# LSTM with a residual: 114 single-pass full-array matmuls on a tile of zeros, and element operations on that tile

## The chip, the core and the metric

The kernel runs on one core of a Trainium2 chip. The metric is the device time of one execution in microseconds (us). The core has five engines that run their own instruction streams and wait for each other by semaphores: PE (TensorE, matrix products into the PSUM memory), DVE (VectorE), ACT (ScalarE), POOL (GpSimd) and SP (which issues most DMA transfers here). PEld is PE's weight load, which can run beside its matmuls.

## The reference

An LSTM over T = 512 steps for a batch of 32, with 512 inputs and 512 hidden units; its output is added to its input. All data are float32.

```python
xW = jnp.einsum('ntd,dg->ntg', x, Wx) + b
def step(carry, xw_t):
    prev_h, prev_c = carry
    a = xw_t + prev_h @ Wh
    i = sigmoid(a[:, :Hd]); f = sigmoid(a[:, Hd:2*Hd]); o = sigmoid(a[:, 2*Hd:3*Hd])
    g = tanh(a[:, 3*Hd:])
    next_c = f * prev_c + i * g
    next_h = o * tanh(next_c)
    return (next_h, next_c), next_h
...
x = x + lstm(x, h0, Wx, Wh, b)
```

## The kernel before

The steps of the recurrence depend on each other, so the kernel is one loop over t = 0 to 511. The batch of 32 fills only 32 of the 128 columns of PE's array; four products, one for each quarter of the hidden units (j = 0 to 3), therefore run side by side, each in its own group of 32 columns, and write 32 of the 128 partitions of a PSUM bank of 512 float32 columns. Each such f32 product shows in the trace as two records of a matmul and two of a weight load.

In step t, `h_part(t)` (L201 to L212) adds h times Wh to the bank of that step: 4 slices of h times 4 quarters, 16 products of 512 columns. `cell(t)` (L214 on) then applies the gates: ACT reads the bank (L225 to L227) and computes tanh of c (L232), DVE forms c and h (L229, L230, L234) and transposes h (L236) into `ht`, one of two buffers, which the next step's `h_part` reads. POOL adds x to `ht` (L244) into `oc`, a tile with room for two steps; every second step SP stores it (L248). In the last eight steps DVE does this addition.

The bank of step t, `bank_of(t)`, is one of two (`gbank`) in all but the first and last steps. Before `h_part(t)` it is seeded with the products of x and Wx of that step by an ACT copy (`seed_step`, L585), which is emitted one step ahead.

Those products of x and Wx come in three ways. The first 24 steps and the last 8 use plain products (`plain_block`, L159). The 480 steps between are made in 20 groups of 24 steps by a scheme with fewer products and more sums: 20 slots of 7 products of 256 columns each per group, a stream of products that `emit_matmuls` (L461 on, the matmul at L477) hands out, some 23 a step, between `h_part(t)` and `h_part(t+1)`, so that PE has work while the gates of step t are computed. Sums of weights go to DRAM early (`vdram`) and come back row by row into `vring`; sums of x are made by DVE in `ubuf` (L388); the products are taken out of five banks `xbank` and one `bbank` by ACT and DVE (`evacuate`, L516 on) into `cbuf`, added up there by DVE (L353), stored to DRAM (`xwd`) and loaded again step by step (`load_xw`, L565).

The order of all instructions on each engine is written out by hand (`manual_schedule`); the Tile framework only adds the waits. `room["dve"]` is a budget that decides in which step DVE does which sum.

At the head, DVE clears `sring` and `tanh_c` (L719, L720), SP loads x, Wx, the bias, h0 and Wh in this order, and PE runs twelve warm-up products on the zeros of `tanh_c` (L742) while it waits. Then PE computes the plain blocks of steps 0 to 4, DVE makes the eight `tail_sums` of the weights (L605 to L608) and adds the bias to five banks (L755), and the loop begins.

Of the kernel before, what the change touches and what calls it, by code (L numbers as in the profile page):

```python
# [6 lines left out]

F32 = mybir.dt.float32
AF = mybir.ActivationFunctionType
PSUM = bass.MemoryType.PSUM  # L10
DRAM = bass.MemoryType.DRAM

P = 128
B = 32
T = 512
NJ = 4
# [72 lines left out]
def kernel(  # L89
# [10 lines left out]
    nc = tc.nc  # L100
    add, sub = nc.vector.tensor_add, nc.vector.tensor_sub

    const = ctx.enter_context(tc.tile_pool(name="const", bufs=1))
    work = ctx.enter_context(tc.tile_pool(name="work", bufs=1))
    dram = ctx.enter_context(tc.tile_pool(name="dram", bufs=1, space=DRAM))
    psum = ctx.enter_context(tc.tile_pool(name="psum", bufs=1, space=PSUM))

    xbank = [psum.tile([P, W], F32, name=f"xbank_{i}") for i in range(5)]
    bbank = psum.tile([P, W], F32, name="bbank")
    gbank = [psum.tile([P, W], F32, name=f"gbank_{i}") for i in range(2)]  # L110

    NC = 11
    r1 = const.tile([P, 8, 4, HW], F32, name="r1")
    cbuf = const.tile([P, NC, 4, HW], F32, name="cbuf")
    r2 = cbuf[:, 0:8]
    wh_sb = const.tile([P, NJ, NJ, W], F32, name="wh_sb")
    vring = const.tile([P, 3, 7, HW], F32, name="vring")
# [23 lines left out]
    def x_of(t):  # L141
        return xnat[:, xslot(t // TC), t % TC]
# [34 lines left out]
    tanh_c = work.tile([P, P], F32, name="tanh_c")  # L177
    hbuf = work.tile([P, P], F32, name="hbuf")
    htr = [work.tile([P, NJ, B], F32, name=f"ht_{i}") for i in range(2)]
    ocr = [work.tile([P, 2, NJ, B], F32, name=f"oc_{i}") for i in range(2)]  # L180
    x_last = vring[:, 0, 0, 0:P]
    h_init = htr[1]
    state["ht"] = h_init
    HALVES = [slice(0, H), slice(H, P)]
# [3 lines left out]
    def is_split(t):  # L188
        return t >= SPLIT

    def bank_of(t):
        if t < KEPT:
            return [gbank[0], gbank[1], xbank[3], xbank[4], xbank[0]][t]
        return gbank[t % 2]

    def half_of(t, i):
        if is_split(t):
            return PAIRS[t % 2][i][:, 0:HW]
        return bank_of(t)[:, i * HW : (i + 1) * HW]
# [14 lines left out]
    def cell(t):  # L214
        n, tt = divmod(t, TC)
        s, nxt = sring[t % 2], sring[(t + 1) % 2]
        o = oring[0]
        ht = htr[t % 2]
        by_gate = lambda a: a.rearrange("p (h g u) -> p h g u", g=G, u=H)
        for part in [(0,), (1,)] if is_split(t) else [(0, 1)]:  # L220
            i = slice(part[0], part[-1] + 1)
            units = slice(H * part[0], H * (part[-1] + 1))
            g = by_gate(half_of(t, part[0])) if is_split(t) else by_gate(bank_of(t))
            for n_, u in enumerate(part):
                nc.scalar.activation(s[:, u, 0:2], g[:, n_, 0:2], AF.Sigmoid)  # L225
                nc.scalar.activation(s[:, u, 2], g[:, n_, 3], AF.Tanh)  # L226
            nc.scalar.activation(o[:, i], g[:, :, 2], AF.Sigmoid)  # L227
            for u in part:
                nc.vector.tensor_mul(prod[:, u], s[:, u, 0:2], s[:, u, 2:4])  # L229
                add(nxt[:, u, 3], prod[:, u, 0], prod[:, u, 1])  # L230
            for u in part:
                nc.scalar.activation(tanh_c[:, HALVES[u]], nxt[:, u, 3], AF.Tanh)  # L232
            for u in part:
                nc.vector.tensor_mul(hbuf[:, HALVES[u]], o[:, u], tanh_c[:, HALVES[u]])  # L234
                if t < T - 1:
                    nc.vector.transpose(ht[:, 2 * u : 2 * u + 2].rearrange("p q b -> p (q b)"), hbuf[:, HALVES[u]])  # L236
            if t == T - 1:
                add(tanh_c[:, units], hbuf[:, units], x_last[:, units])
                nc.sync.dma_start(out=out[n][:, tt * P + units.start : tt * P + units.stop], in_=tanh_c[:, units])
        if t == T - 1:  # L240
            return
        state["ht"] = ht
        oc = ocr[t // 2 % 2]
        (nc.gpsimd if t < T - 8 else nc.vector).tensor_add(oc[:, tt % 2], x_of(t), ht)  # L244
        if tt % 2 == 1 or t == T - 2:
            m = tt % 2 + 1
            stores.append(
                lambda: nc.sync.dma_start(  # L248
                    out=out[n][:, (tt + 1 - m) * P : (tt + 1) * P],
                    in_=oc[:, 0:m].rearrange("p t q b -> p (t q b)"),  # L250
                )
            )
            if t == T - 2:
                stores.pop()()
# [43 lines left out]
    def group(g):  # L298
        if g not in groups:
            groups[g] = Group(g)  # L300
        return groups[g]
# [159 lines left out]
    def emit_matmuls(n):  # L461

        while n > 0 and pos[0] < 4 * len(items):
            i, q = divmod(pos[0], 4)
            row, slot, r = items[i]
            gr, s = group(slot // R), slot % R
            xb = xbank[slot % 5]
            if q == 0 and any(f in finished for f in needs(slot, r)):
                evacuate()
            if r == 2:  # L470
                dst = bbank[:, slot % 2 * HW : (slot % 2 + 1) * HW]
            elif r in (5, 3):
                dst = xb[:, HW:W]
            else:
                dst = xb[:, 0:HW]
            start = r == 2 or (r == 1 and s not in BIAS_OF)
            nc.tensor.matmul(  # L477
                dst[q * B : (q + 1) * B],
                left_of(gr, s, r)[:, q * B : (q + 1) * B],
                vring[:, row % 3, RIGHT[r]],  # L480
                start=start,
                stop=True,
                skip_group_check=True,
            )
            pos[0] += 1
            n -= 1
            if q == 3:
                finished.append((slot, r))
                if r == 4:
                    left_done(gr, s)  # L490

    def needs(slot, r):
        if r == 1:
            return ((slot - 5, 4),)
        if r == 2:
            return ((slot - 2, 2),)
        return {5: (), 6: ((slot, 5),), 3: ((slot, 5),), 7: ((slot, 3),), 4: ((slot, 7),)}[r]
# [18 lines left out]
    def evacuate():  # L516
        for slot, r in finished:
            gr, s = group(slot // R), slot % R
            xb = xbank[slot % 5]
            if r == 5:  # L520
                gr.have[s, "c"] = take(free_c)
                t = cbuf[:, gr.have[s, "c"]]
                nc.scalar.copy(t[:, 0:4:3], xb.rearrange("p (n c) -> p n c", n=2))  # L523
                continue
            if r in (1, 6):
                continue
            t = cbuf[:, gr.have[s, "c"]]
            if r == 2:
                add(t[:, 0], bbank[:, slot % 2 * HW : (slot % 2 + 1) * HW], t[:, 0])  # L529
                room["dve"] -= cost_dve(256)  # L530
            elif r == 3:
                nc.scalar.copy(t[:, 1], xb[:, 0:HW])  # L532
                add(t[:, 1], xb[:, HW:W], t[:, 1])  # L533
                room["dve"] -= cost_dve(256)
            elif r == 7:
                add(t[:, 3], xb[:, 0:HW], t[:, 3])  # L536
                room["dve"] -= cost_dve(256)
            else:
                nc.scalar.copy(t[:, 2], xb[:, 0:HW])  # L539
                gr.have[s] = gr.have.pop((s, "c"))  # L540
                ready(gr, s)
        finished.clear()
# [175 lines left out]
    with tc.manual_schedule():  # L718
        nc.vector.memset(sring[0], 0.0)  # L719
        nc.vector.memset(tanh_c, 0.0)  # L720
        nc.scalar.activation(hbuf, tanh_c, AF.Sigmoid)
        load_x(0, 0, 5)
        for c in range(4):
# [16 lines left out]
        for n in range(3):  # L740
            for j in range(NJ):
                nc.tensor.matmul(  # L742
                    xbank[1 + n % 2][j * B : (j + 1) * B],
                    tanh_c[:, 0:B],
                    tanh_c.unsqueeze(1).to_broadcast([P, 4, P]),
                    start=True,
                    stop=True,
                )
        for c in range(4):
            for t in range(KEPT):  # L750
                plain_block(t, c, bank_of(t))
# [25 lines left out]
        for t in range(T):  # L777
# [6 lines left out]
            c, rest = divmod(t + 6, TC)  # L784
# [14 lines left out]
            if t < HEAD_STEPS:  # L799
# [6 lines left out]
                n = 4 * int((target - done_work) / PROD + 0.5) if n_plain == HEAD - KEPT else 0  # L806
                if t == HEAD_STEPS - 1 and n:
                    n = R * 7 * 4 - pos[0]
# [57 lines left out]
            n = max(0, target - pos[0])  # L866
# [21 lines left out]
            if t >= SPLIT - 9 and late_loads:  # L888
                late_loads.pop(0)()
            emit_matmuls(n)  # L890
            kept_late = []
            for _ in range(0 if t < SPLIT - 2 else 2 if t < SPLIT else 1):
                if plain_tail:
                    p, c = plain_tail.pop(0)
# [60 lines left out]
```

## Time and profile before

| | |
|---|---|
| time, median of 2 runs | 3154.43 us (3153.47 and 3155.4) |
| span of the profiled execution, first to last instruction | 3148.0 us |
| granted PE clock, mean | 0.999 |
| PE busy | 3119.0 us (99%) |
| DVE busy | 2232.8 us (71%) |
| ACT busy | 1454.6 us (46%) |
| POOL busy | 235.6 us (7%) |
| DMA moved | 766.66 MB, mean 244 GB/s |

The profiled execution is one of its own; the page gives its span, and no total time beside it. In the rows, times are in us unless marked ns; "128*32 128x512" is a matmul of 128 rows and 32 columns of weights with 512 moving columns. "[1.55 <-DMA ...]" is the engine's idle time ahead of a row, and what ended it. In the groups of instructions, the count stands behind x, then the busy time in us and the mean of one in ns, then the idle time ahead of them in us. In a view by windows, each stretch has the busy time of each engine and the number of its instructions, then the granted PE clock, the DMA engines' busy share and GB/s. The addition on POOL (L244) comes once a step, so it counts the steps; that of step 39 starts at 358.48 us and that of step 55 at 454.81 us.

### The profile page before, as it was taken

The numbers are of one execution on the slowest core, as the hardware profiler recorded it, in microseconds if no ns is written. First come the engines' busy times: TensorE is split into PE (matmuls) and PEld (weight loads), VectorE is DVE, ScalarE is ACT, GpSimd is POOL, SyncE is SP. The second block draws the span as 40 slices with busy tenths as digits, with TensorE's granted clock in tenths as the row PEclk, the third lists the DMA queues.
The fourth block names the chain that finished last, engine by engine and source line by source line (L and its number), as shares of the span: only waits on it lengthen the run. The fifth ranks groups of instructions, "written<-read, shape, count | busy, mean of one in ns | idle before, by whom it ended". The sixth has DMA issues, their size and how long they took to land.

```text
span 3148.0 us, 105007 instructions
## 1 busy us (share of the span) xinstructions
PE 3119.0 (99%) x41944; PEld 1616.1 (51%) x41944; DVE 2232.8 (71%) x6217; ACT 1454.6 (46%) x5481; POOL 235.6 (7%) x511
## 2 busy tenths in 40 slices
PE   9899999999999999999999999999999999999998
PEld 6544555555555555555555555555555555555465
DVE  5687777767676777777776767777777768677644
ACT  1244444444444444444444444444444444444444
POOL 0000000000000000000000000000000000000000
PEclk9999999999999999999999999999999999999999
DMA  8888777777877777777778777777777777777831
GB/s 290 286 284 269 241 257 243 248 256 247 262 226 254 249 260 241 259 241 249 257 244 265 231 249 251 261 243 251 243 253 257 245 259 231 250 255 235 270 94 37
DMA packets 310808, 766.66 MB, mean 244 GB/s; under 512 B 49392, under 2 KB 92144, under 8 KB 309808
## 3 DMA queue, kind: packets, MB, share of 16 engines
q1 hardware_dynamic: 296800, 740.82, 71.9%
q10 hardware_dynamic: 13280, 18.35, 1.6%
q8 instruction: 331, 5.42, 0.7%
q14 instruction: 157, 1.29, 0.1%
q0 software_dynamic: 240, 0.79, 0.1%
HBM read 577.04 MB, written 182.71 MB: 241 GB/s over the span
## 4 chain that ended last, share of the span: by engine, by line
PE 94%; DVE 3%; DMA 2%; issue 1%; ACT 1%; SPq 0%; POOL 0%; DVEq 0%; ACTq 0%; POOLq 0%
PE gbank L210 52%; PE xbank L477 31%; PE bbank L477 5%; PE xbank L159 2%; PE xbank L210 2%; DVE cbuf L353 1%; PE bbank L159 1%; DMA r<-in_L_cond_Wx_dram 0%; DMA xw<-xwd 0%; DMA xs<-in_L_cond_Wx_dram 0%; DVE prod L229 0%; DVE ubuf L388 0%; DMA vring<-vdram 0%; DVE s L230 0%; DMA r<-in_L_cond_b_dram 0%
## 5 line engine op out<-in xcount | busy, mean ns | idle before, releaser
L210 PE MATMUL gbank<-wh_sb,ht 128*32 128x512 f32 (+1 forms) x16288 | 1792.7, 579 | 6.9 <-DVE ht L236 2.3
L210 PEld LDWEIGHTS gbank<-wh_sb,ht 128*32 128x32 f32 x16288 | 615.0, 110 | 905.7 <-issue 727.1
L477 PE MATMUL xbank<-vring,ubuf 128*32 128x256 f32 x14400 | 932.8, 379 | 10.7 <-DVE ubuf L388 5.9
L225 ACT ACTIVATE s<-gbank 128x128 f32<-128x128 f32 x984 | 275.9, 281 | 1291.5 <-PE gbank L210 1270.9
L477 PEld LDWEIGHTS xbank<-vring,ubuf 128*32 128x32 f32 x14400 | 560.7, 110 | 377.0 <-issue 179.1
L229 DVE TENSOR_TENSOR prod<-s 128x128 f32<-128x128 f32 x1024 | 293.8, 287 | 648.6 <-ACT s L226 648.1
L353 DVE TENSOR_TENSOR cbuf<-cbuf 128x1024 f32<-128x1024 f32 x480 | 581.2, 1218 | 3.9
L244 POOL TENSOR_TENSOR oc<-xnat,ht 128x128 f32<-128x128 f32 x504 | 233.7, 464 | 2874.3 <-DVE ht L236 1601.3
L232 ACT ACTIVATE tanh_c<-s 128x64 f32<-128x64 f32 x1024 | 262.0, 257 | 278.8 <-DVE s L230 273.6
L236 DVE STREAM_TRANSPOSE ht<-hbuf 128x64 f32<-128x64 f32 x1022 | 250.8, 245 | 74.4 <-DVE hbuf L234 0.9
L585 ACT COPY gbank<-xw 128x512 f32<-128x512 f32 x473 | 284.1, 601 | 0.1
L230 DVE TENSOR_TENSOR s<-prod 128x64 f32<-128x64 f32 x1024 | 230.2, 225 | 35.3
L523 ACT COPY cbuf<-xbank 128x512 f32<-128x512 f32 x400 | 233.8, 585 | 40.8 <-PE xbank L477 27.2
L234 DVE TENSOR_TENSOR hbuf<-o,tanh_c 128x64 f32<-128x64 f32 x1024 | 213.2, 208 | 27.2 <-ACT tanh_c L232 26.1
L226 ACT ACTIVATE s<-gbank 128x64 f32<-128x64 f32 x984 | 226.6, 230 | 0.0
L533 DVE TENSOR_TENSOR cbuf<-xbank,cbuf 128x256 f32<-128x256 f32 x400 | 164.0, 410 | 79.0 <-ACT cbuf L532 74.8
L477 PE MATMUL bbank<-vring,ubuf 128*32 128x256 f32 x2400 | 192.3, 379 | 0.6 <-DVE cbuf L529 0.6
L477 PE MATMUL xbank<-vring,xs 128*32 128x256 f32 x2400 | 172.3, 381 | 0.8 <-DVE cbuf L533 0.5
L477 PE MATMUL xbank<-vring,r 128*32 128x256 f32 x2400 | 171.6, 379 | 0.1
L529 DVE TENSOR_TENSOR cbuf<-bbank,cbuf 128x256 f32<-128x256 f32 x400 | 162.0, 405 | 2.7 <-PE bbank L477 2.7
L536 DVE TENSOR_TENSOR cbuf<-xbank,cbuf 128x256 f32<-128x256 f32 x400 | 162.5, 406 | 0.0
L539 ACT COPY cbuf<-xbank 128x256 f32<-128x256 f32 x400 | 145.3, 363 | 20.4 <-PE xbank L477 11.1
(84 smaller groups left out, 1585.4 us busy)
## 6 DMA issues: line engine op xcount, KB each, us to landing
vring<-vdram SPq DMA_DIRECT2D x340, 896.0 KB, 5.9
xwd<-cbuf SPq DMA_DIRECT2D x240, 512.0 KB, 7.1
xw<-xwd SPq DMA_DIRECT2D x1920, 64.0 KB, 3.7
out_dram<-oc SPq DMA_DIRECT2D x255, 128.0 KB, 2.8
xnat<-in_x_dram SPq DMA_DIRECT2D x63, 512.0 KB, 5.0
xs<-in_x_grouped_dram SPq DMA_DIRECT2D x10, 1536.0 KB, 10.6
vring<-vdram SPq DMA_DIRECT2D x20, 768.0 KB, 6.6
r<-in_x_grouped_dram SPq DMA_DIRECT2D x10, 1536.0 KB, 10.3
```

Of the source, the lines that this page charges most:

```text
L210: nc.tensor.matmul(dst[j * B : (j + 1) * B], state["ht"][:, k], m, start=False, stop=True, skip_group_check=True)
L225: nc.scalar.activation(s[:, u, 0:2], g[:, n_, 0:2], AF.Sigmoid)
L226: nc.scalar.activation(s[:, u, 2], g[:, n_, 3], AF.Tanh)
L229: nc.vector.tensor_mul(prod[:, u], s[:, u, 0:2], s[:, u, 2:4])
L230: add(nxt[:, u, 3], prod[:, u, 0], prod[:, u, 1])
L232: nc.scalar.activation(tanh_c[:, HALVES[u]], nxt[:, u, 3], AF.Tanh)
L236: nc.vector.transpose(ht[:, 2 * u : 2 * u + 2].rearrange("p q b -> p (q b)"), hbuf[:, HALVES[u]])
L244: (nc.gpsimd if t < T - 8 else nc.vector).tensor_add(oc[:, tt % 2], x_of(t), ht)
L353: op(c_of(dst), c_of(src), c_of(bb))
L477: nc.tensor.matmul(dst[q * B : (q + 1) * B], left_of(gr, s, r)[:, q * B : (q + 1) * B], vring[:, row % 3, RIGHT[r]], start=start, stop=Tru ...
L523: nc.scalar.copy(t[:, 0:4:3], xb.rearrange("p (n c) -> p n c", n=2))
L585: nc.scalar.copy(bank_of(t), src)
```

## The change

A new tile `zr` of 128 x 256 zeros has the type float32r, a 32-bit float type of PE's; `zf` is the same memory seen as float32, and `zr2` shows its 256 columns twice, which makes 512. To make room, the two output tiles `oc_0` and `oc_1` become one. At the head, behind the warm-up products, 18 matmuls of the full 128 x 128 array work on it (512, 256 and 128 moving columns, six of each), followed by three rounds of element operations on 256, 128 and 64 columns by ACT, DVE (three) and POOL (two). In each of the steps 40 to 47 four, and in each of the steps 48 to 55 eight matmuls of 512 columns are added behind `emit_matmuls`, and add zeros to the bank of the next step. In steps 60 to 75 POOL does two operations on the tile per step. All of it computes with zeros.

```diff
+F32R = mybir.dt.float32r
+MUL, ADD = mybir.AluOpType.mult, mybir.AluOpType.add
...
-    ocr = [work.tile([P, 2, NJ, B], F32, name=f"oc_{i}") for i in range(2)]
+    ocr = [work.tile([P, 2, NJ, B], F32, name=f"oc_{i}") for i in range(1)]
...
+    zr = const.tile([P, 256], F32R, name="zr")
+    zf = zr.bitcast(F32)
+    zr2 = zr.unsqueeze(1).to_broadcast([P, 2, 256])
...
-        oc = ocr[t // 2 % 2]
+        oc = ocr[0]
...
         nc.vector.memset(tanh_c, 0.0)
+        nc.vector.memset(zf, 0.0)
...
+        for n in range(18):
+            cols = (512, 256, 128)[n // 6]
+            nc.tensor.matmul(
+                xbank[1 + n % 2][:, 0:cols],
+                zr[:, n % 2 * P : (n % 2 + 1) * P],
+                zr2 if cols == 512 else zr[:, 0:cols],
+                start=True,
+                stop=True,
+            )
+        for cols in (256, 128, 64):
+            c = slice(0, cols)
+            nc.scalar.activation(zr[:, c], zf[:, c], AF.Copy, scale=1.0 + 2.0**-13)
+            nc.vector.tensor_scalar_mul(zr[:, c], zf[:, c], 1.0 + 2.0**-13)
+            nc.vector.tensor_sub(zr[:, c], zf[:, c], zf[:, c])
+            nc.vector.scalar_tensor_tensor(zr[:, c], zf[:, c], 4096.0, zf[:, c], MUL, ADD)
+            nc.gpsimd.tensor_scalar_mul(zr[:, c], zf[:, c], 1.0 + 2.0**-13)
+            nc.gpsimd.tensor_sub(zr[:, c], zf[:, c], zf[:, c])
...
             emit_matmuls(n)
+            if 40 <= t < 56:
+                for i in range(4 if t < 48 else 8):
+                    nc.tensor.matmul(
+                        bank_of(t + 1), zr[:, i % 2 * P : (i % 2 + 1) * P], zr2, start=False, stop=True, skip_group_check=True
+                    )
+            if 60 <= t < 76:
+                c = slice(0, (256, 256, 128, 64)[(t - 60) // 4])
+                nc.gpsimd.tensor_sub(zr[:, c], zf[:, c], zf[:, c])
+                nc.gpsimd.tensor_scalar_mul(zr[:, c], zf[:, c], 4096.0)
```

## The prediction

> **What bounds the kernel now.** I began with the page of the profiled execution: its totals, then the chain of work that ended last, by engine and by line.
>
> ```profile
> span 3148.0 us, 105007 instructions
> PE 3119.0 (99%) x41944; PEld 1616.1 (51%) x41944; DVE 2232.8 (71%) x6217; ACT 1454.6 (46%) x5481; POOL 235.6 (7%) x511
> PE 94%; DVE 3%; DMA 2%; issue 1%; ACT 1%; SPq 0%; POOL 0%; DVEq 0%; ACTq 0%; POOLq 0%
> PE gbank L210 52%; PE xbank L477 31%; PE bbank L477 5%; PE xbank L159 2%; PE xbank L210 2%; DVE cbuf L353 1%; PE bbank L159 1%; DMA r<-in_L_cond_Wx_dram 0%; DMA xw<-xwd 0%; DMA xs<-in_L_cond_Wx_dram 0%; DVE prod L229 0%; DVE ubuf L388 0%; DMA vring<-vdram 0%; DVE s L230 0%; DMA r<-in_L_cond_b_dram 0%
> ```
>
> PE is busy 99% of the span and is 94% of the chain, almost all of it in two lines: the recurrent products (L210) and the streamed products (L477). An average over stages could hide slack just where the change works, so I looked at the stretch of steps 40 to 55, from the POOL addition of step 39 to that of step 55, and at that of steps 60 to 75, in the busy time by windows; then at PE's groups in the first of these.
>
> ```profile
> core 0: us, PE busy (x) PEld busy (x) DVE busy (x) ACT busy (x) POOL busy (x), PEclk, DMA share, GB/s
> 358.48:454.81 96.33, 96.32 (x1272) 48.99 (x1265) 69.02 (x194) 46.01 (x173) 7.37 (x17) 1.00 0.77 248
> 478.99:575.23 96.24, 96.24 (x1264) 48.95 (x1260) 66.18 (x193) 46.23 (x174) 7.83 (x17) 1.00 0.79 256
> L210 PE MATMUL gbank<-wh_sb,ht 128*32 128x512 f32 x516 | 58.9, 593 | 0.0
> L477 PE MATMUL xbank<-vring,ubuf 128*32 128x256 f32 x464 | 30.3, 379 | 0.0
> ```
>
> In steps 40 to 55 PE is busy 96.32 of 96.33 us at the full granted clock, with no idle time before either group. Matmul ends are modelled, though, so busy may hide small waits. The chain in order of time gives PE's real pace:
>
> ```profile
> 364.56 3.43 PE gbank L210 x32
> 361.97 2.59 PE xbank L477 x48
> ```
>
> 32 records of 512 columns take 3.43 us. Four records, one for each column group of 32, run side by side, so a set of four takes 4 x 3.43 / 32 = 0.429 us; records of 256 columns take half (2.59 / 48 x 4 = 0.216). In the window 516 long and 756 short records at 0.1072 and 0.0536 us make 55.3 + 40.5 = 95.8 us. So waits hide at most 0.5 us there. Work put on PE in these steps lengthens the run by its whole length.
>
> **The change, part by part.**
>
> *The matmuls in steps 40 to 55.* Eight steps get 4 and eight get 8: 96 matmuls of 512 columns over the full 128 x 128 array, each with other weights than the one before. The trace has no full-array matmul and none of this type. An f32 matmul here is two records (16 in h_part, 32 records in the row above). Splitting both factors into a high and a low part gives four products, so I read a record as two passes and estimate one pass of 512 columns at 0.429 / 2 = 0.2144 us. 96 x 0.2144 = **20.6 us**. If instead a record were one pass, it would be 41.2 us, and if the type saved nothing against f32 (two records), 82.3 us; both are rivals below. I take the lowest because the operation is a single pass and the f32 one is two records for four products. The Trainium skill, page "FP8 and Floating Point Precision", section "TensorE Precision Notes", has the same four passes for true FP32 and reads a "reduced precision" FP32 as one truncated operand; no run here shows the latter.
>
> *Their weights.* Each matmul loads 128 columns of weights. Two rows of weight loads in one step:
>
> ```profile
> 400.89 0.16 PEld L210 LDWEIGHTS gbank<-wh_sb,ht 128*32 128x32 f32 x4 [0.27 <-issue]
> 401.32 0.16 PEld L210 LDWEIGHTS gbank<-wh_sb,ht 128*32 128x32 f32 x4 [0.27 <-issue]
> ```
>
> Four loads of 32 columns, 128 columns in all, take 0.16 us, inside the 0.43 us that the set before them is streaming, though they replace weights of the same column groups. 0.16 is under 0.2144, so the loads hide: I take 0. Uncovered they would cost 96 x 0.16 = 15.4 us.
>
> *The change of array shape.* PE goes from column groups of 32 to the full array and back once in each of 16 steps. No row shows such a change. Below, it costs 0; above, each of the 32 changes exposes a matmul's latency beyond its streaming (593 - 429 = 0.164 us) and a load (0.11 us), 8.8 us. The nearest row is the latency, and I take it once for each step (the way back, where weights are ready, hides): 16 x 0.164 = **2.6 us**. The Trainium skill, page "TensorEngine Tiling (Array Packing)", section "Tiling Modes", says that changing the tiling mode, not just the tile, drains the engine; by it both ways pay, a rival below. That speaks against this change, and no row of this trace can confirm it.
>
> *Waits of these matmuls.* They add into the bank of step t+1, which ACT seeds (L585) before cell(t)'s own activations, so that is done during h_part(t). No engine reads it before h_part(t+1). The additional PE time comes where ht is being made, so it takes no cover away.
>
> *The head.* The chip waits there for the first weights, then PE runs the plain blocks and DVE the tail sums:
>
> ```profile
> 5.02 1.68 PE L742 MATMUL xbank<-tanh_c 128*32 128x512 f32 x8
> 8.26 1.97 PE L159 MATMUL gbank<-r,xnat 128*32 128x256 f32 x32 [1.55 <-DMA r<-in_L_cond_Wx_dram]
> 8.14 1.23 DVE L605 TENSOR_TENSOR cbuf<-r 128x1024 f32<-128x1024 f32 x1 [6.60 <-DMA r<-in_L_cond_Wx_dram]
> 19.46 1.23 DVE L608 TENSOR_TENSOR cbuf<-r,cbuf 128x1024 f32<-128x1024 f32 x1
> 22.37 0.70 DVE L755 TENSOR_TENSOR gbank<-gbank,bias_full 128x512 f32<-128x512 f32 x1 [1.68 <-PE gbank L159]
> 25.52 3.81 PE L210 MATMUL gbank<-wh_sb,ht 128*32 128x512 f32 x32
> 31.42 0.25 DVE L236 STREAM_TRANSPOSE ht<-hbuf 128x64 f32<-128x64 f32 x1
> 31.75 0.46 POOL L244 TENSOR_TENSOR oc<-xnat,ht 128x128 f32<-128x128 f32 x1 [31.29 <-DVE ht L236]
> ```
>
> The 18 matmuls, six each of 512, 256 and 128 columns, take 6 x (0.2144 + 0.1072 + 0.0536) = 2.25 us from 6.70 on, to 8.95; 1.55 us of that fills PE's wait. So PE is 0.7 us late. (The warm-up's last two sets take 1.68 us, 0.84 each, about twice the later pace; at that pace the 18 would take 4.5 us and PE be 2.9 us late.) Then come the element operations, 18 in one chain over three engines because all work on the same columns. Their prices, from the groups by shape:
>
> ```profile
> L532 ACT COPY cbuf<-xbank 128x256 f32<-128x256 f32 x400 | 148.5, 371 | 3.9 <-PE xbank L477 2.5
> L227 ACT ACTIVATE o<-gbank 128x128 f32<-128x128 f32 x475 | 146.4, 308 | 0.0
> L232 ACT ACTIVATE tanh_c<-s 128x64 f32<-128x64 f32 x1024 | 262.0, 257 | 278.8 <-DVE s L230 273.6 <-DVE prod L229 4.5 <-DVE hbuf L234 0.5
> L694 DVE TENSOR_TENSOR seeds_own<-seeds_own 128x256 f32<-128x256 f32 x2 | 0.8, 418 | 0.0
> L229 DVE TENSOR_TENSOR prod<-s 128x128 f32<-128x128 f32 x1024 | 293.8, 287 | 648.6 <-ACT s L226 648.1
> L230 DVE TENSOR_TENSOR s<-prod 128x64 f32<-128x64 f32 x1024 | 230.2, 225 | 35.3
> L244 POOL TENSOR_TENSOR oc<-xnat,ht 128x128 f32<-128x128 f32 x504 | 233.7, 464 | 2874.3 <-DVE ht L236 1601.3 <-issue 1044.4 <-DMA xw<-xwd 217.4
> ```
>
> DVE stands in that chain until its last operation of the third round, and the tail sums are queued behind it. ACT 0.371 + 0.308 + 0.257 = 0.94; DVE 3 x (0.418 + 0.287 + 0.225) = 2.79; POOL, two rounds of two, 2 x (0.80 + 0.46) = 2.52 (256 columns lie between 0.46 and 0.93; I take 0.80); seven handovers at 0.08 (31.67 to 31.75) = 0.56; 6.8 in all. From 9.1 that ends at 15.9. Eight tail sums at 1.225 end at 25.7 instead of 20.7, the first bias addition (L755) at 26.4, and h_part(0), which needs it, starts at about 26.5 instead of 25.52: **+1.0 us**, and PE's own 0.7 lies inside it. The steps after it are led by PE, so it stays. Bounds: 0.7, if the element operations are quicker; 5, if POOL takes twice as long (+2.5) and the matmuls run at the slow pace (+2.2). ACT has nothing else to do before cell(0), and the additional memset on DVE lies under the warm-up.
>
> *POOL in steps 60 to 75.* Two operations in each step, at most about 0.9 us each. POOL's rows there:
>
> ```profile
> 484.76 0.46 POOL L244 TENSOR_TENSOR oc<-xnat,ht 128x128 f32<-128x128 f32 x1 [5.31 <-issue]
> 490.79 0.46 POOL L244 TENSOR_TENSOR oc<-xnat,ht 128x128 f32<-128x128 f32 x1 [5.56 <-DVE ht L236]
> ```
>
> They wait for nothing and lie in 5.3 us of idle time: 0. Were DVE slowed by them through all 1.8 us of a step, by half, that is 0.9 us of DVE's slack of (96.24 - 66.18) / 16 = 1.9; only what falls into cell() would count, up to 4 us over 16 steps.
>
> *One output buffer instead of two.* The addition of an even step now waits until the store of the pair before has landed. In steps 60 to 75, then in the last steps, where DVE does that addition:
>
> ```profile
> L248 SPq DMA_DIRECT2D out_dram<-oc x9: 338/345/365, 479.5 to 575.1; - x9
> DMA to landing us min/median/max: 1.7/2.8/6.1
> 3119.05 0.33 SPq L248 DMA_DIRECT2D out_dram<-oc  x1
> 3123.08 0.29 DVE L244 TENSOR_TENSOR oc<-xnat,ht 128x128 f32<-128x128 f32 x1
> DMA to landing us min/median/max: 1.7/1.7/1.9
> ```
>
> The store goes out some 0.5 us after the odd addition and lands 2.8 us later; the next even addition comes a step (5.8 us) on. A landing of 6.1 makes POOL about a microsecond late, and the ht that it reads is overwritten only two steps later, so nobody waits. On SP, the store stands before the loads of x and xw, but it waits for the odd addition as before. In the last steps a landing of 1.9 ends at 3121.0, before 3123.08. 0; with landings of 6.1 there, DVE would lose 2.1 us in each of three pairs, 6 us.
>
> *Sum.* 20.6 + 2.6 + 1.0 = 24.2 us on a span of 3148.0: 3172.2. The two runs shown have a median of 3154.43, 6.4 above the span, which I take for what lies around it: **3178.6 us**, 0.8% slower.
>
> **The rivals.**
>
> *Every change of shape drains.* For: PE holds several matmuls in flight (593 ns against a pace of 429). Against: sets follow each other here without a gap, weights included. 32 x 0.164 = 5.2 instead of 2.6: 3181.2.
>
> *A matmul costs about twice as much.* Either a record is one pass (0.429 each, 41.2 us) or each full-array matmul shows its latency (0.214 + 0.164 = 0.378, 36.3 us). For: no row separates a pass from a record. Against: four products in two records. 41.2 + 2.6 + 1.0 = 44.8: 3199.2.
>
> *Slower beyond 2%: the full f32 price.* If the full array is fed this type at f32's rate, a matmul costs 0.857, 82.3 us: 82.3 + 3.6 = 85.9, 3240.3 us (2.7%). It decides from (63.1 - 3.6) / 96 = 0.62 us a matmul on. For: the operands have 4 bytes as f32 has. Against: single pass.
>
> *Not slower.* The matmuls would have to fill time in which PE only seems busy, in the 16 steps: ht arriving after the streamed products end. It decides from about 1.3 us a step; the rows leave 0.5 us in all sixteen. If it held all, 3155.4.
>
> **How the numbers follow.** Forecast 0.46; a drain both ways 0.25; twice the price 0.18; full f32 price 0.07; not slower 0.02; 0.02 for something else, such as late stores. 3178.6 is the first. The range goes from below the forecast's own lower bound (20.6 + 0 + 0.7 on 3154.4 is 3175.7), with a few us for the head's waits falling otherwise, to above the doubled price with a late head (3199.2 + 4): 3170 to 3203. It leaves out the full f32 price and not slower. Two per cent is 63 us, about what a measurement of this kernel can tell from no change; all cases but the full f32 price lie within: faster 0.01, within 0.92, slower 0.07.
>
> **What would show it.** In the changed profile: 114 new matmul records on the full array, one for each, not two; 96 of them some 0.214 us apart, back to back; the stretch of steps 40 to 55 about 23 us longer, and that of steps 60 to 75 within 1 us of 96.2; h_part(0) starting at about 26.5 us; no wait of POOL or DVE on the output stores worth a microsecond on PE. A spacing of 0.38 or 0.43 means the doubled price, 0.86 the full one. A gap of 0.16 on both sides of each group means drains both ways. If the total grows by over 30 us while spacing and gaps are as forecast, the cost lies in the head or the stores, and I am wrong there.

## The result, and the profile after

The changed kernel takes 3177.99 us (median of 2 runs, 3176.9 and 3179.09) against 3154.43: ratio 1.0076, 95% interval 1.0046 to 1.0105. Over five rounds it was 3177.69 against 3152.1, ratio 1.0078 (1.0065 to 1.0090), that is 20 to 28 us. It is slower, by less than 2%. The profiled execution has a span of 3175.0 us, 27.0 more than that of before. The page of the changed kernel (its line numbers are higher: h_part is L215, the stream L482, the added matmuls L757 at the head and L916 in the steps):

```profile
span 3175.0 us, 105267 instructions
PE 3147.5 (99%) x42058; PEld 1628.2 (51%) x42058; DVE 2238.7 (71%) x6227; ACT 1456.1 (46%) x5484; POOL 269.1 (8%) x549
PE 95%; DVE 3%; DMA 1%; ACT 1%; issue 0%; SPq 0%; POOL 0%; DVEq 0%; ACTq 0%; POOLq 0%
```

PE's busy time grew by 28.5 us, its records by 114: one for each added matmul. The busy time by windows shows where the span grew: the 16 steps from step 40 on, first before, then after, then the after window cut between step 47 and step 48.

```profile
364.49:460.83 96.34, 96.33 (x1264) 48.58 (x1259) 68.84 (x194) 46.42 (x175) 7.37 (x16) 1.00 0.80 262
```

```profile
365.20:488.35 123.15, 123.15 (x1360) 56.13 (x1360) 68.91 (x194) 46.84 (x175) 7.34 (x17) 1.00 0.66 211
365.20:423.09 57.89, 57.89 (x669) 25.11 (x665) 34.63 (x97) 23.50 (x88) 3.67 (x8) 1.00 0.67 216
423.09:488.35 65.26, 65.26 (x696) 31.02 (x696) 34.28 (x98) 23.34 (x88) 3.68 (x9) 1.00 0.64 206
```

123.15 - 96.34 = 26.8 us of the 27.0 lie in these steps, with PE busy throughout. Step 40 begins 0.7 us later than before (365.20 against 364.49). That is about what the head costs, but in the kernels below that have the same head it begins anywhere from 362.71 (bfloat16 in column groups) to 367.19 (spread), so one execution can't give the head's price there. The eight steps with four matmuls take 57.89 us and those with eight 65.26; before, both halves took about 48.17. So four matmuls lengthen a step by 9.72 / 8 = 1.21 us and eight by 17.09 / 8 = 2.14. The difference gives 0.23 us for a matmul, and about 0.3 us is left for each step, whatever their number. The timeline and the view of the tile show where it lies:

```profile
364.63 0.64 PE L482 MATMUL xbank<-vring,ubuf 128*32 128x256 f32 x8
365.21 1.20 PE L916 MATMUL gbank<-zr 128*128 128x512 f32 x4
366.33 3.64 PE L215 MATMUL gbank<-wh_sb,ht 128*32 128x512 f32 x32
423.09 2.11 PE L916 MATMUL gbank<-zr 128*128 128x512 f32 x8
425.13 3.64 PE L215 MATMUL gbank<-wh_sb,ht 128*32 128x512 f32 x32
365.20 0.76 PEld L916 LDWEIGHTS gbank<-zr 128*128 128x128 f32 x4 [0.41 <-issue]
365.31 0.19 PEld L916 LDWEIGHTS gbank<-zr 128*128 128x128 f32 x1
L916 PE MATMUL gbank<-zr x96: 387/397/504, 365.2 to 481.9; 128*128 128x512 f32 x96
```

Two sets of streamed matmuls start at 364.63; at their pace of 0.216 us a third would start at 365.06, and the first full-array matmul starts at 365.21, 0.15 later. Four of them then last 1.12 us to the first matmul of h_part, eight last 2.04: 0.23 each, and 0.20 beyond that. So a group costs 0.35 us beside its matmuls; in the step times some 0.3 is left of it, since the added work also fills waits that were there before (0.7 us in the 16 steps, as the column groups below show). The longest record, 504 ns against 397, is the first of a group. Its weights begin to load only with it (365.20 against 365.21), and the next load begins 0.11 us later (365.31, the second of the four): about 0.1 of the 0.20 is the first matmul's wait for its own weights.

### The profile page after: what moved, and what is told of

It reads as the page before. It is cut to its first block, busy times and chain, and to the rows that moved or that the text cites. A ratio compares the mean times of both kernels' runs of the same rounds, so it can differ in the third digit from the quotient of the medians.

```text
span 3175.0 us, 105267 instructions
## 1 busy us (share of the span) xinstructions
PE 3147.5 (99%) x42058; PEld 1628.2 (51%) x42058; DVE 2238.7 (71%) x6227; ACT 1456.1 (46%) x5484; POOL 269.1 (8%) x549
## 4 chain that ended last, share of the span: by engine, by line
PE 95%; DVE 3%; DMA 1%; ACT 1%; issue 0%; SPq 0%; POOL 0%; DVEq 0%; ACTq 0%; POOLq 0%
PE gbank L215 52%; PE xbank L482 31%; PE bbank L482 5%; PE xbank L161 2%; PE xbank L215 2%; DVE cbuf L358 1%; PE gbank L916 1%; PE bbank L161 1%; DMA vring<-vdram 0%; DVE prod L234 0%; DVE ubuf L393 0%; DVE s L235 0%; DMA r<-in_L_cond_b_dram 0%; PE gbank L161 0%; DMA vdram<-cbuf 0%
## 5 line engine op out<-in xcount | busy, mean ns | idle before, releaser
L215 PE MATMUL gbank<-wh_sb,ht 128*32 128x512 f32 (+1 forms) x16288 | 1792.8, 579 | 7.2 <-DVE hbuf L239 2.3
L215 PEld LDWEIGHTS gbank<-wh_sb,ht 128*32 128x32 f32 x16288 | 612.0, 110 | 909.5 <-issue 733.1
L482 PE MATMUL xbank<-vring,ubuf 128*32 128x256 f32 x14400 | 932.2, 379 | 10.5 <-DVE ubuf L393 5.6
L482 PEld LDWEIGHTS xbank<-vring,ubuf 128*32 128x32 f32 x14400 | 558.5, 110 | 378.8 <-issue 179.7
L482 PE MATMUL bbank<-vring,ubuf 128*32 128x256 f32 x2400 | 192.1, 379 | 0.6 <-DVE cbuf L534 0.6
L482 PE MATMUL xbank<-vring,xs 128*32 128x256 f32 x2400 | 171.8, 380 | 0.9 <-DVE cbuf L538 0.5
L482 PE MATMUL xbank<-vring,r 128*32 128x256 f32 x2400 | 171.6, 379 | 0.1
```

The source lines that it names most:

```text
L215: nc.tensor.matmul(dst[j * B : (j + 1) * B], state["ht"][:, k], m, start=False, stop=True, skip_group_check=True)
L482: nc.tensor.matmul(dst[q * B : (q + 1) * B], left_of(gr, s, r)[:, q * B : (q + 1) * B], vring[:, row % 3, RIGHT[r]], start=start, stop=Tru ...
```

## Experiments

**More rounds of the same kernel.**

> The changed kernel once more, with more timed rounds. Theory: the trace's account holds for the times too, span of after minus span of before: 3175.0 - 3148.0 = +27.0 us, ratio about 1.0086. Rival: the prediction's sum, +24.2 us, ratio 1.0077, and the profiled execution of before was a quick one. With 5 rounds the interval may or may not part the two; the stretch of steps 40 to 55 in the profile should again take 123.2 us (365.20 to 488.35) against 96.3.

Ratio 1.0078 (1.0065 to 1.0090) against both expectations, 1.0086 and 1.0077: the times do not part them. The stretch did come back:

```profile
366.16:489.32 123.16, 123.16 (x1360) 56.20 (x1360) 68.92 (x194) 46.84 (x175) 7.37 (x17) 1.00 0.66 210
```

Before runs between 3148.8 and 3157.5 us over all executions, so the whole time is blunt here, and the stretches of the trace, which here repeated to 0.01 us, carry what follows. The kernels below for which no ratio is given ran once, and their profile is read alone.

**One matmul in each of 96 steps.**

```diff
-            if 40 <= t < 56:
-                for i in range(4 if t < 48 else 8):
+            if 40 <= t < 136:
+                for i in [t]:
```

> The same 96 matmuls, but one in each of the steps 40 to 135 instead of 4 or 8 in each of 16. Theory (every step that holds such matmuls pays about 0.3 us for the change of array shape, beside 0.231 us a matmul): 96 x (0.23 + 0.30) = 51 us over before, some 3205 us, spread evenly over 96 steps. Rival (the 26.8 us are a price for each matmul, 0.28 us, whatever its neighbours): 27 us over before, as in the changed kernel.

3199.03 us, ratio 1.0144 (1.0129 to 1.016). The 96 steps in the windows, before and with the spread matmuls:

```profile
364.49:941.15 576.66, 576.36 (x7560) 293.17 (x7555) 421.10 (x1172) 276.85 (x1034) 44.20 (x97) 1.00 0.77 250
```

```profile
367.19:993.12 625.93, 625.93 (x7656) 254.11 (x7656) 424.22 (x1172) 278.16 (x1034) 75.66 (x128) 1.00 0.72 230
```

49.3 us more, 0.51 for each step with one matmul (0.5 us of it are POOL's operations in steps 60 to 75, below). The whole time grew by 46.9, near it within what executions differ by. The theory's 51 nearly holds, and the price per matmul alone (27) falls.

**All 96 in one step.**

```diff
-            if 40 <= t < 56:
-                for i in range(4 if t < 48 else 8):
+            if t == 48:
+                for i in range(96):
```

> The same 96 matmuls all in step 48. Theory (0.3 us for each step that holds them): 96 x 0.231 + 0.3 = 22.5 us in that one step, 4.3 us less than the changed kernel's 26.8. Rival (a price for each matmul): 26.8 us in that step. Both can be read from the start of the POOL additions of steps 48 and 49.

POOL's additions of steps 48 and 49:

```profile
414.08 0.46 POOL L249 TENSOR_TENSOR oc<-xnat,ht 128x128 f32<-128x128 f32 x1 [5.55 <-DVE ht L241]
442.24 0.46 POOL L249 TENSOR_TENSOR oc<-xnat,ht 128x128 f32<-128x128 f32 x1 [27.69 <-DVE ht L241]
```

The step takes 28.16 us instead of 6.04 (412.64 to 418.68 before): 22.1 more for 96 matmuls, against 22.5 by the theory and 26.8 by the rival. The time is 3174.48 us, ratio 1.0065 (1.0051 to 1.0079). So the number of visits costs, beside the number of matmuls.

**The same matmuls in float32.**

```diff
+    zf2 = zf.unsqueeze(1).to_broadcast([P, 2, 256])
...
-                        bank_of(t + 1), zr[:, i % 2 * P : (i % 2 + 1) * P], zr2, start=False, ...
+                        bank_of(t + 1), zf[:, i % 2 * P : (i % 2 + 1) * P], zf2, start=False, ...
```

> The 96 matmuls of steps 40 to 55 read the same zeros as float32 instead of float32r. Theory (f32 takes four passes in two records, float32r one): two records a matmul, 0.43 us each, 96 x 0.86 + 16 x 0.3 = 87 us over before in these steps, slower by 2.8%. Rival (a record is one pass, so f32 takes two): 96 x 0.43 + 5 = 46 us.

3238.09 us, ratio 1.0269 (1.0255 to 1.0283). PE's group, and the 16 steps:

```profile
L917 PE MATMUL gbank<-zr 128*128 128x512 f32 x192 | 86.7, 601 | 0.0
366.53:549.81 183.28, 183.28 (x1456) 74.64 (x1456) 68.90 (x194) 46.81 (x175) 7.29 (x16) 1.00 0.43 141
```

192 records, two a matmul, and 183.28 - 96.34 = 86.9 us (theory 87). An f32 record takes 0.43 us on the full array as on column groups, and a float32r record a little over half of that: an f32 record is worth two passes of 512 columns. This is the price that the rival "full f32 price" would have brought, and float32r does not pay it.

**bfloat16 on the full array, and in column groups.** Both read the zeros as bfloat16; the second cuts each matmul into four of 32 weight columns.

```diff
+    zb = zr.bitcast(mybir.dt.bfloat16)
...
-                        bank_of(t + 1), zr[:, i % 2 * P : (i % 2 + 1) * P], zr2, start=False, ...
+                        bank_of(t + 1), zb[:, i % 2 * P : (i % 2 + 1) * P], zb, start=False, ...
```

```diff
+                    for j in range(NJ):
+                        nc.tensor.matmul(
+                            bank_of(t + 1)[j * B : (j + 1) * B],
+                            zb[:, i % 2 * P + j * B : i % 2 * P + (j + 1) * B],
+                            zb,
...
```

> The 96 matmuls of steps 40 to 55 read the same zeros as bfloat16 (512 of them), still on the full array. Theory (the surplus over one pass, 0.231 against 0.2144 us a matmul, and half of the step's 0.3 us come from the load of 128 columns of 4-byte weights; the rest is the change of shape): with 2-byte weights a pace of 0.216, a gap in front of the group still 0.31, and 20.7 + 16 x 0.2 = 24 us more in these steps. Rival (all of it is the change of shape and the array's own pace): 26.8 as with float32r.

> As the bfloat16 kernel, but each full-array matmul is cut into four with 32 columns of weights each, side by side in the column groups that the neighbours use, so the shape of the array never changes; the same columns stream. Theory (the change of shape costs): no gap in front or behind, 96 x 0.2144 = 20.6 us, less up to 0.8 us of hidden waits, in these steps. Rival (the gaps belong to the change of type or to matmuls that add to the bank of the next step): about 24 us, with the gap of 0.31 in front.

The 16 steps with the full array and then with column groups, each with a first group of four and its neighbours (L917 and L918 are the added matmuls); for the full array also the group of step 48. In the trace of the full array one matmul record of each group is missing:

```profile
366.13:486.27 120.14, 119.30 (x1344) 47.44 (x1360) 68.88 (x194) 46.79 (x175) 7.29 (x16) 1.00 0.67 216
365.56 0.64 PE L483 MATMUL xbank<-vring,ubuf 128*32 128x256 f32 x8
366.14 1.04 PE L917 MATMUL gbank<-zr 128*128 128x512 bf16 x3
367.11 1.92 PE L216 MATMUL gbank<-wh_sb,ht 128*32 128x512 f32 x16
422.75 1.90 PE L917 MATMUL gbank<-zr 128*128 128x512 bf16 x7
424.58 0.64 PE L216 MATMUL gbank<-wh_sb,ht 128*32 128x512 f32 x4
366.13 0.55 PEld L917 LDWEIGHTS <-zr 128*128 128x128 bf16 x4 [0.41 <-issue]
366.15 0.10 PEld L917 LDWEIGHTS <-zr 128*128 128x128 bf16 x1
```

```profile
362.71:478.94 116.23, 116.23 (x1648) 63.22 (x1641) 68.91 (x194) 46.82 (x175) 7.34 (x17) 1.00 0.69 221
367.73 1.94 PE L483 MATMUL xbank<-vring,ubuf 128*32 128x256 f32 x32
369.46 1.07 PE L918 MATMUL gbank<-zr 128*32 128x512 bf16 x16
370.32 0.64 PE L216 MATMUL gbank<-wh_sb,ht 128*32 128x512 f32 x4
369.24 0.79 PEld L918 LDWEIGHTS <-zr 128*32 128x32 bf16 x16
```

Full array: 23.8 us more than before (theory 24, rival 26.8). Column groups: 19.9 (theory 20.6 less up to 0.8; rival 24). In the timeline of the latter the sets follow without a gap: 8 sets of 0.216 from 367.73 end at 369.46, and 4 sets of 0.215 at 370.32; their weights begin to load 0.22 us ahead of them (369.24). On the full array the gap in front is 0.15 us as with float32r (two sets from 365.56 on end at 365.99, the first matmul starts at 366.14), and the weights again begin only with it. Four matmuls last 0.97 us to h_part and eight 1.83: 0.216 each and 0.10 beyond. So the same columns cost 19.9 us in the neighbours' shape, 3.9 more on the full array (0.24 us for each of 16 visits), and another 3.0 with float32r. Of these 3.0, 0.1 us for each group is the load of the first weights: the second load begins 0.11 us after the first with float32r and 0.02 after it with bfloat16. The rest is the pace, 0.231 against 0.216; bfloat16 halves the bytes of the weights and of the moving operand alike, so this pair does not say which of the two sets it.

**Without the 96 matmuls.**

```diff
-            if 40 <= t < 56:
-                for i in range(4 if t < 48 else 8):
-                    nc.tensor.matmul(...)
```

> The changed kernel without the 96 matmuls of steps 40 to 55; the head, POOL's operations and the one output buffer stay. Theory: only the head costs, +0.7 to 1.0 us, steps 40 to 55 take 96.3 us and steps 60 to 75 96.2 as before; ratio 1.000 within the interval. Rival (POOL's operations or the one buffer cost too): 2 to 6 us more, in steps 60 to 75 or in the last eight steps.

3152.56 us, ratio 0.9996 (0.9987 to 1.0005): all the rest of the change is within 0.13% of nothing. The 15 steps from step 40 on, before and here:

```profile
364.49:454.81 90.32, 90.31 (x1192) 45.85 (x1187) 64.10 (x181) 43.42 (x163) 6.91 (x16) 1.00 0.79 255
```

```profile
366.60:456.87 90.27, 90.27 (x1192) 46.09 (x1187) 63.90 (x181) 43.59 (x163) 6.89 (x16) 1.00 0.79 250
456.87 0.46 POOL L249 TENSOR_TENSOR oc<-xnat,ht 128x128 f32<-128x128 f32 x1 [5.56 <-DVE ht L241]
464.80 1.25 POOL L249 TENSOR_TENSOR oc<-xnat,ht 128x128 f32<-128x128 f32 x1 [7.47 <-DMA out_dram<-oc]
468.69 0.46 POOL L249 TENSOR_TENSOR oc<-xnat,ht 128x128 f32<-128x128 f32 x1 [2.64 <-DVE ht L241]
```

The single output buffer does make POOL wait: its addition of step 56 is held until a store has landed and comes 1.9 us late; the next is back in time, and PE sees none of it. In this kernel nine of POOL's waits end with a landed store.

**The head without the element operations.** The three rounds of ACT, DVE and POOL operations are left out, and the 18 matmuls stay.

> The changed kernel without the 18 element operations at the head; its 18 matmuls stay. Theory (PE's own delay by the 18 matmuls sets the head): h_part(0) starts at 26.5 us as in the changed kernel, though DVE is done with the tail sums by 20.7 again. Rival (the prediction: the chain on DVE sets it): h_part(0) starts at 26.2 us or earlier, 0.7 us behind before or less.

The head of the changed kernel, then without the chain:

```profile
6.33 2.99 PE L757 MATMUL xbank<-zr 128*128 128x512 f32 x18
9.25 1.97 PE L161 MATMUL gbank<-r,xnat 128*32 128x256 f32 x32
16.12 1.22 DVE L610 TENSOR_TENSOR cbuf<-r 128x1024 f32<-128x1024 f32 x1
24.45 1.23 DVE L613 TENSOR_TENSOR cbuf<-r,cbuf 128x1024 f32<-128x1024 f32 x1
25.59 1.29 DVE L778 TENSOR_TENSOR gbank<-gbank,bias_full 128x512 f32<-128x512 f32 x2
26.54 3.69 PE L215 MATMUL gbank<-wh_sb,ht 128*32 128x512 f32 x32
```

```profile
6.65 2.99 PE L757 MATMUL xbank<-zr 128*128 128x512 f32 x18
9.57 1.97 PE L161 MATMUL gbank<-r,xnat 128*32 128x256 f32 x32
23.71 0.70 DVE L770 TENSOR_TENSOR gbank<-gbank,bias_full 128x512 f32<-128x512 f32 x1 [2.11 <-PE gbank L161]
26.86 3.69 PE L215 MATMUL gbank<-wh_sb,ht 128*32 128x512 f32 x32
```

Without the chain, h_part(0) starts at 26.86, 0.32 later than with it, as its 18 matmuls do (6.65 against 6.33). In both, PE runs from the first plain block to h_part(0) without a gap, 17.29 us. So PE's own delay sets the head; the chain on DVE fits under it.

**Without POOL's operations in steps 60 to 75.**

```diff
-            if 60 <= t < 76:
-                c = slice(0, (256, 256, 128, 64)[(t - 60) // 4])
-                nc.gpsimd.tensor_sub(zr[:, c], zf[:, c], zf[:, c])
-                nc.gpsimd.tensor_scalar_mul(zr[:, c], zf[:, c], 4096.0)
```

> The changed kernel without POOL's two operations in each of the steps 60 to 75. In the changed kernel the 16 steps from the POOL addition of step 60 on take 96.4 us (before: 95.9), half a microsecond of it in steps 64 to 66. Theory (POOL's operations slow DVE, and so a step): 95.9 us again. Rival (the one output buffer, or chance): 96.4 us still.

These 16 steps and DVE's costliest group over some 105 us there, in the changed kernel and without POOL's operations:

```profile
512.23:608.60 96.37, 96.04 (x1264) 48.76 (x1260) 66.42 (x191) 45.95 (x172) 29.41 (x46) 1.00 0.81 261
L358 DVE TENSOR_TENSOR cbuf<-cbuf 128x1024 f32<-128x1024 f32 x16 | 20.9, 1305 | 0.2
```

```profile
513.09:608.95 95.86, 95.85 (x1264) 48.92 (x1259) 64.88 (x191) 46.08 (x173) 7.37 (x17) 1.00 0.80 262
L358 DVE TENSOR_TENSOR cbuf<-cbuf 128x1024 f32<-128x1024 f32 x17 | 20.7, 1217 | 0.2
```

95.86, as before the change (95.88), so POOL's operations cost 0.5 us. With them DVE's sums take 1305 ns instead of 1217 on average, and PE is idle for 0.33 us of the stretch instead of 0.01; the one wait of PE that the profile names there is for DVE.

**128 moving columns instead of 512.**

```diff
-                        bank_of(t + 1), zr[:, i % 2 * P : (i % 2 + 1) * P], zr2, ...
+                        bank_of(t + 1)[:, 0:P], zr[:, i % 2 * P : (i % 2 + 1) * P], zr[:, 0:P], ...
```

> The 96 matmuls of steps 40 to 55 with 128 moving columns instead of 512. Theory (the load of 128 columns of weights sets a floor of 0.113 us a matmul, as the narrow matmuls of the head suggest): 96 x 0.113 + 16 x 0.34 - 0.7 = 15.5 us more in these steps. Rival (the loads are hidden at every width, as the prediction had it): 96 x 0.054 + 16 x 0.34 - 0.7 = 9.9 us.

```profile
364.82:475.59 110.77, 110.77 (x1360) 51.27 (x1360) 68.89 (x194) 46.80 (x175) 7.30 (x17) 1.00 0.73 233
418.41 1.11 PE L916 MATMUL gbank<-zr 128*128 128x128 f32 x8
419.45 1.06 PE L215 MATMUL gbank<-wh_sb,ht 128*32 128x512 f32 x8
```

14.4 us more than before: nearer to the floor by the weight load (15.5) than to hidden loads (9.9). The eight matmuls of step 48 last 1.04 us to h_part, the four of step 40 0.59 (364.82 to 365.41): 0.11 each. A quarter of the columns costs 14.4 / 26.8 = 54% of the time.

## Why the prediction was right, and where it was not

The time, 3178.6 forecast and 3178.0 measured, is closer than its working deserves: two errors of about 3 us cancel, and that is luck. The span grew by 27.0 us where 24.2 was forecast, and what lies around the span is 3.0 us (3177.99 - 3175.0) where 6.4 was. On the span, the rival "every change of shape drains" (20.6 + 5.2 + 1.0 = 26.8) was nearer than the forecast, and its sign, a gap of about 0.16 us on both sides of a group, came nearest to what the trace shows.

- *PE bounds these steps, so added work lengthens them by its whole length*: shown. In the neighbours' shape the 96 passes cost 19.9 of their 20.6 us; the missing 0.7 are hidden waits that they fill (at most 0.5 forecast).
- *One pass of 512 columns is 0.2144 us, half an f32 record*: shown, by 0.215 in column groups and by the float32 run's 86.9 us. The rivals "twice" and "full f32 price" fall.
- *Weight loads hide, 0*: mis-sized. The first matmul of each group waits about 0.1 us for its weights, which are not loaded ahead of it (16 x 0.1 = 1.6). The pace is 0.231 us instead of 0.2144; against bfloat16's 0.216 that is another 96 x 0.015 = 1.4. That this too is the load is argued, not shown: 128 columns don't come faster than 0.11 us each, but a float32 record of 0.43 us hides a load of the same 4-byte weights wholly. The row used, 0.16 us for four loads of 32 columns, was that of four column groups side by side, and no row had a load behind a change of shape.
- *The change of shape, once a step, 2.6 us*: mis-sized. Both ways pay, 3.9 us by the bfloat16 pair, about 0.15 into the full array and 0.1 behind it. That is the rival "every change of shape drains", which had 5.2 us. The Trainium skill, page "TensorEngine Tiling (Array Packing)", section "Tiling Modes", says that such a change drains the engine; the trace agrees as far as it shows a gap on both sides on the full array and none in column groups.
- *The head, +1.0 us by the chain on DVE*: the size was right (26.54 against the 26.5 forecast), the reason wrong. The 18 matmuls start at 6.33 (6.70 forecast) and the first plain block behind them at 9.25 (8.95 forecast): they take 2.92 us instead of 2.25, as matmuls of 128 columns come no faster than 0.11 us apart. So PE arrives at h_part(0) 1.0 us late by itself. DVE's chain ended at 16.2 (forecast 15.9), just early enough.
- *POOL's operations, 0 to 4 us, taken as 0*: 0.5 us, the way that the bound had it, through DVE. *One output buffer, 0*: shown; POOL waits for stores, and nobody waits for POOL.
- *What lies around the span, 6.4 us*: wrong. In the changed kernel the profiled execution took 3176.9 us, 1.9 above its span of 3175.0, and every execution on record took 1.7 to 2.2 us beside its span. The rest of the 6.4 was the distance of a quick profiled execution from the median of two others.

The 27.0 us of the span are: steps 26.8 (forecast 23.2), step 40 reached 0.7 later, POOL 0.5, and 1.0 less elsewhere, within what executions differ by; where between the head and step 40 the head's 1.0 shrinks to 0.7 was not traced.

## What to carry to other kernels

On an engine that is busy all the time, price added matmuls by passes times columns, and then count the visits: each group in another array shape paid 0.24 us here with bfloat16 and 0.34 with float32r, so 96 matmuls cost 22 us in one step, 27 in 16 and 49 in 96. Cut into the shape that the neighbours use, the same work had no gap. A price for overhead is best read as a difference between two stages of one trace, since whole times here wander by several us.

## What the runs showed of the hardware that was not expected

- Narrowing the float32r matmuls from 512 to 128 columns saved only 46% of the time. They did not come faster than about 0.11 us each, twice what a quarter of a pass takes; that the load of 128 columns of weights sets this floor fits (a load follows the first of a group by 0.11 us, too), and no run separates it from other floors.
- POOL's multiplication by a constant took longer than its subtraction of two tiles on the same 256 columns: mean 1358 against 612 ns in steps 60 to 67, though it reads one operand. At the head, where DVE stands still meanwhile, the single one on 256 columns took 848 ns.

```profile
L922 POOL TENSOR_SCALAR zr<-zr 128x256 fp32r<-128x256 f32 x8 | 10.9, 1358 | 0.7
L921 POOL TENSOR_TENSOR zr<-zr 128x256 fp32r<-128x256 f32 x8 | 4.9, 612 | 0.0
```
